# Queries of three kv groups by Strassen's scheme, and scores two steps ahead, in a decoder layer on one core

## The chip, the cores and the metric

The kernel runs on one core of one Trainium2 chip. The metric is device time in microseconds (us) of one execution. TensorE is called PE here, VectorE DVE, ScalarE ACT, GpSimd POOL, and SyncE, whose queue issues the DMAs, SP.

## The reference

One decoder layer on 8 sequences of 128 tokens with 512 channels: attention with 32 query heads in 8 kv groups of 4, cross attention with a context, and a gated feed-forward network (FFN) with 4-bit weights. Cut to what the change touches:

```python
def _L0_attn_ref(hidden_states, w_q, w_k, w_v, w_o):
    ...
    q = (hidden_states @ w_q).reshape(B, S, Hkv, g, D)      # 1024 x 512 @ 512 x 4096
    k = (hidden_states @ w_k).reshape(B, S, Hkv, D)
    v = (hidden_states @ w_v).reshape(B, S, Hkv, D)
    scores = jnp.einsum('bqhgd,bkhd->bhgqk', q, k) * scale
    ...
    probs = jax.nn.softmax(scores.astype(jnp.float32), axis=-1).astype(q.dtype)
    attn = jnp.einsum('bhgqk,bkhd->bqhgd', probs, v)
    attn = attn.reshape(B, S, Hq * D)
    return attn @ w_o
...
x = x + _L0_attn_ref(_layernorm(x, axis=-1), L0_attn_w_q, L0_attn_w_k, L0_attn_w_v, L0_attn_w_o)
```

All of it is float32.

## The kernel before

**Three products for one.** A float32 operand is held as two float16 tiles, a high part and the remainder. `split` (L117) makes them: ACT casts the high part, DVE or POOL subtracts it from the source. `mm3` (L160) then runs three matmuls per contraction block of 128: high x high, high x remainder, remainder x high. All accumulate in one PSUM bank.

**Tiling.** The 8 sequences make two halves of 4, that is of 512 tokens. The normalized input stands transposed in `hT`, four contraction blocks of 128 channels by 512 tokens for each half. Weights are fetched from memory per kv group in float32 into a raw tile (`rawq`, one buffer for all groups). ACT sums their squares (`sumsq`, L244), PE and DVE make a scale of it (`scales_parts`, L276). `convert` (L350) multiplies by the scale on POOL in place and splits the result, remainder on POOL.

**Queries.** `proj_q` (L497) computes one head of 128 rows for one half: 4 contraction blocks x 3 matmuls of 512 columns, 12 in all, into a bank of tag `j`; then `split` writes `qh` on ACT and `ql` on DVE. PSUM has two banks for each of four tags (L187): `j` for projections, `s` for scores, `a` for values, `o` for output projections.

**Steps.** A step is one kv group on one sequence; there are 64. A unit is one group on one half, 4 steps; 16 units run group by group (the last two groups take turns by halves). `step(i)` (L1365) issues, in this order:

- `att_s` (L587) for step i+1: 12 matmuls of scores, row maxima on DVE, exponentials on ACT, scaling on POOL (L622), the two float16 parts of the probabilities `pb` (ACT and POOL, L121), and a DMA that transposes `pb` to `pt`
- `proj_piece`: a fourth of the projections of the unit after the next one begun, that is one head's queries, and at times keys or values
- `att_o` (L653) for step i-1: 12 matmuls of 512 columns, then DVE adds the result to the residual `xr` (L662)
- `att_v` (L639) for step i: 5 matmuls of 256 columns with `pt`, then the split to `ah` (ACT) and `al` (DVE)

What else a step does comes from a table `todo`: fetches, sums of squares and weight conversions of later groups, each at a fixed step. Steps 8 to 42 also hold one chunk of the FFN's dequantization each (`dequant`, L785): two loads and two DVE instructions (L807, L811) that write the FFN weights `nf`. From step 43 the context is loaded and prepared, from step 53 another step function mixes in cross attention, and from step 60 the FFN.

**Order.** The order of instructions on each engine is made when the program is built, by a scheduler that follows these issues and some hand-set orders (`issue_after`, L124). Each engine then runs its own list in order; waits between engines are semaphores.

## Time and profile before

| what | us |
|---|---|
| timed runs | 659.69, 659.74, 661.82; median 659.74 |
| the profiled execution | 660.26 |
| its span, first to last instruction | 658.5 |
| PE busy | 631.9 |
| DVE busy | 465.0 |
| ACT busy | 440.0 |
| POOL busy | 378.5 |

The profile comes from one execution. Its lines name the source line, engine, operation and tiles (output <- inputs), and give the count, busy time, mean duration and what ended the idle time before. In lists over time the first number is the start and the second the duration, both in us from the span's start. Durations of matmuls overlap one another. The output projections of steps 8, 16, 24, 32 and 42 are added to `xr` at 117.4, 178.9, 238.3, 298.1 and 376.0 us, so these steps take 7.6 us in the mean.

### The profile page before, as it was taken

Reading aid. Unit: us, or ns where it says so; the run is one execution under the profiler, and the core shown is the slowest. Engines: PE = TensorE matmul, PEld = TensorE weight load, DVE = VectorE, ACT = ScalarE, POOL = GpSimd, SP = SyncE. Lnnn points to the kernel's source line nnn. Section 1 sums busy time; section 2 is a strip of 40 time slices with the busy share of each in tenths; the row PEclk is TensorE's granted clock in tenths of the full one; section 3 lists DMA queues with packets and bytes.
Section 4 is the critical chain, followed back from the end, with each engine's and each line's share of the span. In section 5 each row is a group of like instructions: output and inputs, shape, how many; then the busy total and the mean of one; then the engine's idle time right before and its main releaser. Section 6 shows DMA issues by size and latency. Waiting matters only on the chain.

```text
span 658.5 us, 12421 instructions
## 1 busy us (share of the span) xinstructions
PE 631.9 (96%) x3992; PEld 342.8 (52%) x3992; DVE 465.0 (71%) x1475; ACT 440.0 (67%) x1238; POOL 378.5 (57%) x586
## 2 busy tenths in 40 slices
PE   8799999999999999999999999989998988999996
PEld 5465545565655555555555554546554444445443
DVE  6756776666766777677768554757776768988986
ACT  5587678465658575666668566856566578867674
POOL 7757477563738693464678395724576247622521
PEclk9899999999999999999999999999999999999999
DMA  9277254945553766455455523333544253112002
GB/s 310 53 169 176 67 81 117 230 98 157 127 153 104 183 142 148 123 145 145 130 159 96 136 40 109 70 88 60 90 73 70 40 89 53 24 25 65 1 1 64
DMA packets 117773, 69.34 MB, mean 105 GB/s; under 512 B 84190, under 2 KB 100593, under 8 KB 117708
## 3 DMA queue, kind: packets, MB, share of 16 engines
q1 hardware_dynamic: 117708, 68.55, 44.2%
q8 instruction: 31, 0.51, 0.3%
q14 instruction: 34, 0.28, 0.2%
HBM read 42.12 MB, written 2.20 MB: 67 GB/s over the span
## 4 chain that ended last, share of the span: by engine, by line
PE 62%; DVE 10%; POOL 9%; ACT 8%; DMA 7%; issue 3%; SPq 1%; DVEq 0%; POOLq 0%; ACTq 0%
PE ps_c L1181 6%; PE ps_o L166 6%; PE ps_c L1182 6%; PE ps_o L164 6%; PE ps_o L165 6%; PE ps_q L164 5%; PE ps_q L166 5%; PE ps_q L165 5%; DMA pt<-pb 2%; POOL pb L121 2%; DMA rawq<-in_L_attn_w_q_dram 2%; POOL s L622 2%; ACT junk L262 2%; DVE ps_c L1194 2%; PE ps_k L165 1%
## 5 line engine op out<-in xcount | busy, mean ns | idle before, releaser
L565 ACT ACTIVATE s<-s,negm 128x64 f32<-128x64 f32 (+1 forms) x256 | 93.1, 365 | 41.1 <-DVE negm L608 40.8
L164 PE MATMUL ps_q<-hT,wqh 128*128 128x512 f16 (+1 forms) x260 | 97.7, 376 | 2.6 <-DVE ql L121 1.6
L164 PE MATMUL ps_o<-woh,ah 128*128 128x512 f16 x256 | 97.1, 379 | 3.0 <-ACT ah L118 3.0
L166 PE MATMUL ps_o<-woh,al 128*128 128x512 f16 x256 | 96.9, 379 | 1.1 <-DVE al L121 0.6
L166 PE MATMUL ps_q<-hT,wql 128*128 128x512 f16 (+1 forms) x260 | 97.7, 376 | 0.0
L165 PE MATMUL ps_q<-hT,wqh 128*128 128x512 f16 (+1 forms) x260 | 97.7, 376 | 0.0
L165 PE MATMUL ps_o<-wol,ah 128*128 128x512 f16 x256 | 97.0, 379 | 0.0
L662 DVE SCALAR_TENSOR_TENSOR xr<-ps_o,unsc,xr 128x512 f32<-128x512 f32 x64 | 47.9, 748 | 48.6 <-PE ps_o L166 46.0
L121 POOL TENSOR_TENSOR pb<-s,pb 128x256 f16<-128x256 f32 (+1 forms) x128 | 70.6, 566 | 17.9 <-ACT pb L118 15.5
L575 POOL TENSOR_SCALAR rec<-rec 128x4 f32<-128x4 f32 x64 | 15.2, 237 | 99.0 <-DVE rec L573 77.8
L608 DVE CUSTOM_DVE_ANT_0 s<-ps_sc,mask,soft 128x64 f32<-128x64 f32 (+1 forms) x256 | 67.3, 310 | 3.8 <-PE ps_sc L166 1.4
L121 DVE TENSOR_TENSOR ql<-ps_q,qh 128x512 f16<-128x512 f32 x64 | 44.0, 687 | 33.3 <-ACT qh L118 33.1
L622 POOL TENSOR_TENSOR s<-s,rec 128x128 f32<-128x128 f32 (+1 forms) x128 | 63.5, 517 | 4.7
L118 ACT CAST pb<-s 128x256 f16<-128x256 f32 (+1 forms) x128 | 42.8, 348 | 26.5 <-POOL s L622 24.7
L118 ACT CAST ah<-ps_at 128x512 f16<-128x512 f32 x64 | 37.3, 583 | 24.5 <-PE ps_at L166 9.7
L565 ACT ACTIVATION_READ_ACCUMULATOR s<-s,negm 128x1 f32 x256 | 48.0, 187 | 0.0
L121 DVE TENSOR_TENSOR al<-ps_at,ah 128x512 f16<-128x512 f32 x64 | 43.7, 683 | 4.7 <-ACT ah L118 4.4
L1194 DVE TENSOR_SCALAR ps_c<-ps_c,rTg 128x512 f32<-128x512 f32 (+1 forms) x56 | 40.7, 750 | 7.1 <-PE ps_c L1182 6.8
L118 ACT CAST qh<-ps_q 128x512 f16<-128x512 f32 x64 | 36.6, 572 | 11.7 <-PE ps_q L166 10.6
L1192 ACT ACTIVATE ps_c<-ps_c,rTu 128x512 f32<-128x512 f32 (+1 forms) x57 | 36.3, 660 | 11.3 <-PE ps_c L1182 9.3
L166 PE MATMUL ps_sc<-k,ql 128*128 128x128 f16 (+1 forms) x256 | 42.9, 207 | 0.5 <-DVE ql L121 0.5
L165 PE MATMUL ps_sc<-k,qh 128*128 128x128 f16 (+1 forms) x256 | 41.8, 207 | 0.0
(244 smaller groups left out, 1699.5 us busy)
## 6 DMA issues: line engine op xcount, KB each, us to landing
rawq<-in_L_attn_w_q_dram SPq DMA_DIRECT2D x8, 1024.0 KB
rawo<-in_L_attn_w_o_dram SPq DMA_DIRECT2D x8, 1024.0 KB, 5.8
zi<-zd SPq DMA_DIRECT2D x26, 256.0 KB, 4.1
vd<-v SPq DMA_DIRECT2D x64, 64.0 KB, 3.0
qr<-_L_ffn_down_qweight_dram SPq DMA_DIRECT2D x10, 256.0 KB
xr<-in_x_dram SPq DMA_DIRECT2D x8, 256.0 KB, 8.6
rawk<-in_L_attn_w_k_dram SPq DMA_DIRECT2D x8, 256.0 KB, 5.8
rawv<-in_L_attn_w_v_dram SPq DMA_DIRECT2D x4, 512.0 KB, 6.9
```

Of the source, the lines that this page charges most:

```text
L118: a = nc.scalar.copy(hi, src)
L121: b = (lo_eng or nc.vector).tensor_tensor(lo, src, hi, ALU.subtract)
L164: nc.tensor.matmul(ps, lh, rh, start=start and i == 0, stop=False)
L165: nc.tensor.matmul(ps, lh, rl, start=False, stop=False)
L166: nc.tensor.matmul(ps, ll, rh, start=False, stop=stop and i == n - 1)
L565: exp = nc.scalar.activation(v, v, AF.Exp, bias=negm[:, j : j + 1], scale=-1.0, accum_out=sums[:, j : j + 1],)
L608: nc.vector.tensor_tensor_reduce(view, flat(ps, cols[j]), masks[j // 2], soft_t[g][:, j % 2 : j % 2 + 1], BIG, ALU.add, ALU.min, negm,)
L622: mul = nc.gpsimd.tensor_tensor(v, v, rec[:, 2 * k : 2 * k + 2].unsqueeze(2).to_broadcast([P, 2, (k + 1) * HQ]), ALU.mult,)
L662: return nc.vector.scalar_tensor_tensor(xr[b], ps, unsc_t[g], xr[b], ALU.mult, ALU.add)
L1181: nc.tensor.matmul(ps, lh, rh, start=r == 0, stop=False, skip_group_check=r > 0)
L1182: nc.tensor.matmul(ps, lh, rl, start=False, stop=True, skip_group_check=r > 0)
L1194: nc.vector.tensor_scalar(ps, ps, sc, None, ALU.mult)
```

## The change

**Strassen's scheme.** For kv groups 3 to 5, two heads and one half are computed together. Weights of the two heads form a 2 x 2 block matrix (two heads by two halves of the contraction), the tokens another (two halves of the contraction by 256 tokens left and right). Eight block products become seven, in Winograd's form, on sums of weight blocks and sums of token blocks. Each block product is 2 contraction blocks x 3 matmuls of 256 columns.

- Token sums: `t_sum` makes four differences for each half, once, in steps 8 to 17, into new tiles `T0` and `T1` (DVE for the sum, `split` on ACT and POOL). They are built from a float32 copy of the tokens; that of half 0 is left from the start, that of half 1 is added up again from `hT` by two DVE adds.
- Weight sums: `fast_scale`, `fast_sums` and `fast_cast` work per pair of heads on POOL in place in `rawq`, with casts before and after: 3.5 tile pairs for two heads instead of 2. A plan `FPLAN` spreads them over 5 steps.
- The product itself, `fast_q`, comes in four stages over three steps. Two banks `A` and `B` of tag `j` are held. ACT copies a finished bank to SBUF and half of it back into the other bank, on which PE goes on accumulating; DVE adds twice from one bank half into another, and PE accumulates onto one of these sums.

**Order.** In steps 14 to 42 `att_s` and the projections run two steps ahead instead of one (step 14 issues both, step 42 none). Queries of the three groups are placed by hand before and after `att_o`; their keys and values use banks of tag `o`. Fetches of query weights for groups 3 to 5 come one step earlier than before relative to their use, and weight preparation of groups 3 to 7 is moved one step ahead.

**Memory.** Scratch tiles of the start (`hb`, `zw`, `z`, `srow`, `scol`) now lie inside the FFN weight tiles `nf`, which are filled later. No work is added by that.

The core of the diff:

```diff
+    def t_sum(half, n):
+        full = h32b if half else h32
+        b = [[full[:, 2 * r : 2 * r + 2, c * HH : (c + 1) * HH] for c in range(2)] for r in range(2)]
+        if half and n < 2:
+            ks = slice(2 * n, 2 * n + 2)
+            return nc.vector.tensor_tensor(
+                full[:, ks, :], hT[0][1][:, ks, :], hT[1][1][:, ks, :], ALU.add
+            )
+        dst, one, two, i = (
...
+        ins = nc.vector.tensor_tensor(dst, one, two, ALU.subtract)
+        split(tT[half][:, 0, i], tT[half][:, 1, i], dst, nc.gpsimd)
...
+    def fast_sums(g, p, part):
...
+        tt = nc.gpsimd.tensor_tensor
+        if part == 0:
+            issue_after(tt(a22, a21, a22, ALU.add), pace["mul"])
+            tt(a21, a11, a21, ALU.subtract)
+        else:
+            issue_after(tt(a11, a22, a11, ALU.subtract), pace["mul"])
+            tt(a12, a12, a11, ALU.subtract)
...
+        A = bank("j", [P, TH], "ps_q")
+        m5 = term(A[:, right], Z1, 2, summed(0), True)
+        term(A[:, left], X, 0, tok(0, left), behind=m5)
+        B = bank("j", [P, TH], "ps_q")
+        u = B[:, left]
+        both = work.tile([P, TH], F32, name="s5", tag="s5", bufs=1)
+        nc.scalar.copy(both, A)
+        s5 = both[:, right]
+        nc.scalar.copy(u, both[:, left])
+        yield
+        term(A[:, left], X, 2, tok(2, left))
+        term(u, Z0, 0, summed(1))
+        nc.vector.tensor_tensor(A[:, right], u, s5, ALU.add)
+        yield
+        term(u, Z1, 0, summed(2))
+        nc.vector.tensor_tensor(B[:, right], u, s5, ALU.add)
+        term(A[:, right], Z0, 2, tok(2, right))
+        put_q(g, half, 2 * p, A)
+        yield
+        term(u, Y, 2, summed(3))
+        put_q(g, half, 2 * p + 1, B)
...
+        for p in range(2):
+            i = HB * u - 7 + 2 * p
...
+            place(slot_b, i, go[p])
+            place(slot_b, i + 1, go[p])
+            place(slot_a, i + 2, go[p])
+        place(slot_a, HB * u - 4, lambda g=g, half=half: run(proj_k(g, half, place="o")))
...
+    SOON, BACK = 14, 42
+
     def step(i):
         g, b = steps[i]
-        if i + 1 < len(steps):
+        if i <= SOON or i > BACK:
             att_s(*steps[i + 1])
-        proj_piece(*divmod(i + 1 + HB, HB))
+            proj_piece(*divmod(i + 1 + HB, HB))
+        if SOON <= i < BACK:
+            att_s(*steps[i + 2])
+            proj_piece(*divmod(i + 2 + HB, HB))
+        for f in slot_a.pop(i, ()):
+            f()
         after = att_o(*steps[i - 1]) if i else None
+        for f in slot_b.pop(i, ()):
+            f()
         att_v(g, b)
```

`term(ps, w, k0, rhs)` runs the six matmuls of one block product: two contraction blocks from `k0`, three matmuls each.

## The prediction

> **What bounds the kernel now.** I read four views: the busy shares and slices of the page, the busy times by stage, the timeline of the matmuls, and PE's waits. The profiled execution took 660.26 us, 658.5 of it span. The median of the three timed runs is 659.74; I work against the profile and take 0.5 off at the end.
>
> The page first. PE is near full in every slice until the last third, at full granted clock.
>
> ```profile
> PE 631.9 (96%) x3992; PEld 342.8 (52%) x3992; DVE 465.0 (71%) x1475; ACT 440.0 (67%) x1238; POOL 378.5 (57%) x586
> PE   8799999999999999999999999989998988999996
> PEclk9899999999999999999999999999999999999999
> ```
>
> The stages that the change touches, in busy us (instructions):
>
> ```profile
> 103.00:163.00 60.00, 59.96 (x402) 33.62 (x401) 38.71 (x130) 38.20 (x125) 35.55 (x58) 1.00 0.60 145
> 163.00:223.00 60.00, 60.00 (x399) 33.52 (x397) 40.09 (x139) 39.42 (x129) 39.49 (x62) 1.00 0.54 134
> 223.00:283.00 60.00, 60.00 (x400) 33.57 (x399) 40.96 (x135) 38.13 (x125) 35.73 (x59) 1.00 0.63 152
> 283.00:344.00 61.00, 60.72 (x411) 34.10 (x410) 43.29 (x140) 40.00 (x129) 39.25 (x61) 1.00 0.50 135
> ```
>
> The columns are PE, PEld, DVE, ACT, POOL. PE is full, the others two thirds. But a PE duration overlaps the next one, so full by this count is not yet proof. The timeline settles it (start, duration):
>
> ```profile
> 300.40 0.27 PE L164 MATMUL ps_v<-wvh,hT 128*128 128x256 f16 x1
> 300.51 0.27 PE L165 MATMUL ps_v<-wvl,hT 128*128 128x256 f16 x1
> ...
> 302.49 0.38 PE L165 MATMUL ps_q<-hT,wqh 128*128 128x512 f16 x1
> 302.71 0.38 PE L166 MATMUL ps_q<-hT,wql 128*128 128x512 f16 x1
> ```
>
> What a matmul costs is the step to the next start. Twelve 512-column ones start over 2.37 us (302.28 to 304.65), 0.2155 each; ten 256-column ones over 0.98 (299.75 to 300.73), 0.109 each, every one with a new weight. I summed such steps over the matmuls' sizes and held them against the clock: from 100 to 300 us they fill all but some 0.3 us; from 145 to 436 us about 6 us are missing, 4.9 of them after 376. So in steps 8 to 42 PE's own work is the time, nearly to the last tenth. PE's waits agree:
>
> ```profile
> PE ps_o L164 <- ACT ah L118: 3.0, 3, 1.7
> PE ps_at L645 <- DMA pt<-pb: 1.9, 4, 0.8
> PE ps_q L164 <- DVE v L545: 1.0, 1, 1.0
> ```
>
> Three, four and one waits in the whole run.
>
> **What the change removes on PE.** Three groups, two halves, two pairs of heads make 12 pairs. A pair was 2 x 12 matmuls of 512 columns; it becomes 7 products x 6 matmuls of 256. Off go 288 x 0.2155 = 62.1 us; on come 504 x 0.109 = 54.9. Net 7.2 us, all in a stage where PE has no gap. The built order confirms the counts (288 fewer of 512, 504 more of 256, no other matmul changed), and from step 52 on PE's order is that of before.
>
> The Trainium skill, page "TensorE: Matmul & The Clock Gate", section "Back-to-back issue gap", speaks against this: in streams of weight load and matmul it gives some 81 ns at 128 columns and 131 at 512; halfway (98 at 256, my interpolation) the change would lose 504 x 0.098 - 288 x 0.131 = 11.7 us. The trace has 0.2155 at 512 and 0.109 at 256, which fits the same section's formula for an isolated gap, so I don't follow the 131.
>
> **What it adds elsewhere** (built order for counts, rows of the profile for durations):
> - ACT: 12 copies of a whole bank out of PSUM (row of 128x512 from PSUM, 0.58) 7.0; 12 copies of 256 back into PSUM (128x256 cast, 0.37) 4.5; 6 more casts of 128x512 (0.62) and 6 of 128x256 (0.40) for the weights, 6.1; 8 casts of token sums, 4.9. Together 22.5 us.
> - DVE: 24 adds of 256 with one PSUM input (128x256 row, 0.42) 10.1; 6 token sums (0.72 at 512; two of 1024, about 1.4) 5.7. Together 15.8.
> - POOL: 24 weight sums in place (256-element row, 0.63) 15.1; 12 more weight remainders (6 x 1.20, 6 x 0.68) 11.3; 8 token remainders (1.17) 9.4. Together 35.8.
> - SP: not one DMA more (287 rows in both). The weight fetch of a group moves one step ahead, and waits for POOL's last reading of the one raw buffer; behind it in SP's queue stand the transposes of the probabilities and the dequantization loads.
>
> None of this runs on PE. Its cover is the idle third of the three engines. The token sums lie in steps 8 to 17, the rest in some 185 us (steps 17 to 42). POOL gets 26 us there, from about 63% to 79% (26 less work time of PE counted); ACT goes from 65% to about 76%, DVE from 68% to about 74%. On average everything fits. Were the cover gone, POOL's 26 us would be the price.
>
> It is uneven, though. Summing POOL's rows between the score steps in the built order, eight steps around 17 to 24 hold 53.5 us against some 59 of PE's work, and four in a row 31 against 30; before, the same eight held 41. The heaviest 20 us of before, 320 to 340, had POOL busy 18.6 of 20 and PE without a gap, so such a burst can be carried. Scores two steps ahead give one step more, some 7 us, for POOL, DMA and the softmax; that is the cover for the burst. In time by itself it gives little: the 0.3 us wait for a transpose at 302, perhaps 1.5 us in all with the gaps around 374.
>
> A second effect of a busier POOL is on DVE:
>
> ```profile
> 299.20 1.33 POOL L121 TENSOR_TENSOR wql<-rawq,wqh 128x512 f16<-128x512 f32 x1
> ...
> 299.55 1.52 DVE L811 SCALAR_TENSOR_TENSOR nfd<-qi,zi 128x512 f16<-128x512 int32 x1
> 310.33 0.69 DVE L811 SCALAR_TENSOR_TENSOR nfd<-qi,zi 128x512 f16<-128x512 int32 x1
> ```
>
> The same dequantization step takes 0.69 us alone and 1.52 beside a POOL subtraction. With some five to ten more such meetings DVE loses 3 to 8 us, off the path. The Trainium skill, "SBUF — State Buffer", section "Who interferes with whom", gives the reason (a DVE instruction with two SBUF inputs and a GpSimd one that reads SBUF block each other); by its rule the 24 new adds, with one input in PSUM, stay free, and the token sums do not. I count nothing on PE for either.
>
> **What it adds as waits on PE.** Each pair hands over three times: PE to ACT and back (first two products, then the copies), PE to DVE and back twice. A handover takes what a matmul runs past its step (0.27 - 0.11 = 0.16), the copy (0.58) or add (0.42) and a signal: about 0.8 and 0.65 us if the engine is free, and more by what stands ahead of it in order. In the built order I added PE's own work between producer and consumer: 2 to 5 us nearly everywhere, but 0.6 and 0.7 in two of the copies and 0.5 in one add, and 1.2 to 1.8 in a few. The matmul that waits holds all of PE behind it. With a free engine that is 0.1 to 0.3 us at three places, 0.5 us; with one instruction of 0.6 ahead at six places, some 4 us. Nothing bounds it better: queue lengths at those points are not in this trace. The same kind of handover (queries to scores, values to outputs) costs PE under 2 us in steps 8 to 42 of before, so I take 2.5, from a range of 0.5 to 7.
>
> Behind step 42, six gaps worth 5 us up to 436 us (at 391, 410, 427, 434 and smaller) hang on ACT behind loads of the context and on the preparation of groups 6 and 7, which moves one step. I take them as they are, within 2 either way. From there PE's order is unchanged and follows earlier.
>
> **Sum.** 660.3 - 7.2 - 0.5 (gaps that the lead closes) + 2.5 = 655.1 by the profile, 654.5 by the median.
>
> **Rivals.**
> 1. *New waits eat the gain* (chance 0.24): 5 to 9 us of handovers and late POOL results. For it: in-order engines at 76%, three short distances, bursts on POOL. Against: the near absence of such waits before at similar bursts. 657 to 661; say 659.
> 2. *POOL becomes the bound* (0.10), the slower side. Place: the eight steps of each group's weight preparation. It decides once POOL, with its waits for ACT's casts between its subtractions, can't be busy over about 85% there: 53.5 / 0.85 = 63 us against 59. At 80% it is 67, 8 us lost in the densest eight steps, and about 3 in each of the two others of 44 to 48 us with their own bursts: 659.7 - 7.2 + 14 = 666. For it: over 60 us no stage showed POOL over 44. Against: the 93% over 20 us.
> 3. *The change does less than it says* (0.03): a 256-column matmul costs more than half of a 512 one. By the duration columns (0.379 and 0.273) the change would add 504 x 0.273 - 288 x 0.379 = 28 us. The steps between starts speak against it, on every row of 256.
> 4. *More than forecast* (0.08): handovers cost nothing and the lead also fills the gaps after 376: 7.2 + 2 to 3, 650.
>
> Forecast case 0.55, 652 to 656.4.
>
> **The numbers.** A measurement of this kernel can tell about 0.5%, 3.3 us, from no change. Under 656.4 lie the forecast case, rival 4 and a few hundredths of rival 1: 0.66. Within 3.3 us: most of rival 1 and the mildest of rival 2: 0.25. Slower: the rest of rivals 2 and 3, 0.09. The range takes in rival 4 and rival 1: 650.5 to 661.
>
> **What would show it.** Right: 504 new matmuls at 0.109 us from start to start; the four 60-us windows still full on PE; the end of the last output projection 5 us earlier; POOL near 75 to 80% between 190 and 370 us. Wrong: PE waits on the copy into ps_q, on the adds, or on pt with over 4 us in total (rival 1); gaps of PE that end with POOL or with transposes behind POOL around steps 16 to 24 (rival 2); steps of 256 above 0.12 (rival 3).

## The result, and the profile after

The changed kernel takes **667.71 us** (median of four runs, 667.46 to 669.19) against 659.72 (four runs, 659.36 to 661.82) of the kernel before: a ratio of 1.0125, interval 1.0109 to 1.0140. The forecast was 654.5 in a range of 650.5 to 661, so the sign was wrong too.

The profiled execution after has a span of 665.7 us (658.5 before). The page of the kernel after, in its first rows:

```profile
PE 628.3 (94%) x4208; PEld 364.2 (55%) x4208; DVE 489.1 (73%) x1509; ACT 455.7 (68%) x1282; POOL 424.0 (64%) x630
...
PE   8799999989999989999997799999998988999996
```

PE does less and takes longer. Its row of slices (16.6 us each), nines without a break from 33 to 428 us before, has holes now: eights at 133 and 233 us and two sevens from 349 to 383 us. The stages, same windows and columns as before (PE, PEld, DVE, ACT, POOL, then the granted clock):

```profile
103.00:163.00 60.00, 57.79 (x390) 32.30 (x389) 44.91 (x141) 40.27 (x130) 44.53 (x65) 1.00 0.48 121
163.00:223.00 60.00, 58.04 (x431) 37.09 (x429) 49.26 (x140) 41.91 (x130) 52.61 (x71) 1.00 0.58 147
223.00:283.00 60.00, 56.17 (x477) 40.65 (x474) 41.99 (x140) 41.84 (x137) 45.42 (x70) 1.00 0.54 135
283.00:344.00 61.00, 60.96 (x478) 41.11 (x477) 45.37 (x149) 44.69 (x140) 50.04 (x73) 1.00 0.62 151
344.00:380.00 36.00, 28.50 (x211) 17.55 (x209) 23.21 (x71) 19.16 (x65) 21.27 (x32) 0.95 0.47 132
380.00:440.00 60.00, 60.00 (x407) 33.56 (x406) 37.27 (x156) 45.94 (x149) 42.96 (x66) 1.00 0.27 67
```

Three of the four windows that were full are short by 2 to 4 us, the stretch 344 to 380, at a clock of 0.95, by 7.5; the one from 380 on is full. In the kernel before these last two windows were

```profile
344.00:380.00 36.00, 35.43 (x234) 19.04 (x232) 25.49 (x92) 25.14 (x83) 21.92 (x35) 1.00 0.54 119
380.00:440.00 60.00, 55.89 (x377) 30.56 (x376) 35.05 (x147) 40.62 (x124) 41.25 (x63) 1.00 0.34 82
```

The saving itself came: the timeline of PE in a product of the kernel after has

```profile
203.86 0.27 PE L603 MATMUL ps_q<-hT,wql 128*128 128x256 f16 x1
203.97 0.38 PE L603 MATMUL ps_q<-hT,wqh 128*128 128x256 f16 x2
204.19 0.27 PE L603 MATMUL ps_q<-hT,wql 128*128 128x256 f16 x1
204.30 0.19 PE L164 MATMUL ps_sc<-k,qh 128*128 128x64 f16 x1
```

that is four 256-column matmuls in 0.44 us, 0.11 each.

For all that follows I sum PE's **gaps**: the time between the starts of matmuls in excess of what their columns take (0.2157, 0.109, 0.0557 us for 512, 256, 128). PE's own work fell from 626.2 to 619.5, by some 7 (7.2 by the counts); the gaps rose from 25.5 to 39.5, by 14. (The two levels depend on what the few float32 matmuls of the start are taken for; the differences and the table don't.) By place:

| gaps of PE in us | 100 to 200 | 200 to 380 | 380 to 460 | 100 to 460 |
|---|---|---|---|---|
| before | 0.3 | 1.3 | 5.7 | 7.3 |
| after | 4.8 | 15.3 | 0.3 | 20.4 |

PE's waits, kernel after:

```profile
PE ps_at L770 <- DMA pt<-pb: 10.4, 11, 3.2
PE ps_o L166 <- DVE al L121: 2.9, 5, 1.8
...
PE ps_o L164 <- ACT ah L118: 1.7, 2, 1.1
...
PE ps_sc L166 <- DVE ql L121: 1.5, 2, 1.0
...
PE ps_q L603 <- DVE ps_q L629: 1.3, 2, 0.9
```

DVE's adds of the new handovers (`ps_q`, last row) hold PE for 1.3 us, and this view has no row of a wait on ACT's copies. What holds it for ten is `pt`, the transposed probabilities, 1.9 before; they come at the end of the longest chain (scores, DVE, ACT, POOL, ACT and POOL, SP, DMA). The chain that ended last shows what lies in it, here across the worst gap of the kernel after:

```profile
355.10 0.64 DVE xr L787
355.74 2.04 DVE qi L932
357.78 0.60 DVE ql L121
358.38 3.09 DVE nfd L936
361.46 0.10 DVE rec L698
361.56 0.28 SPq L924
...
361.95 6.29 DMA rawo<-in_L_attn_w_o_dram
```

`qi` and `nfd` are the two DVE instructions of a chunk of the FFN's dequantization. Free they take 0.48 and 0.69 us; here 2.12 and 3.16 by the timeline. Behind them stand DVE's evictions; SP's queue held a load (L924) whose buffer `nfd` frees, then a 1-MB weight fetch, and only then the transpose, whose `pb` was ready at 360. It landed at 368.9, 6.4 us after its issue; the median of those whose landing the profile tells is 3.0. PE waited 3.2 us, until 369.0, and behind the gap its clock was halved, from about 371 to 374.4: a 512-column matmul started every 0.43 us.

### The profile page after: what moved, and what is told of

Its sections match the earlier page's. It is cut to its first block, busy times and chain, and to the rows that moved or that the text cites. A ratio compares the mean times of both kernels' runs of the same rounds, so it can differ in the third digit from the quotient of the medians.

```text
span 665.7 us, 13013 instructions
## 1 busy us (share of the span) xinstructions
PE 628.3 (94%) x4208; PEld 364.2 (55%) x4208; DVE 489.1 (73%) x1509; ACT 455.7 (68%) x1282; POOL 424.0 (64%) x630
## 4 chain that ended last, share of the span: by engine, by line
PE 41%; POOL 18%; DVE 11%; ACT 11%; DMA 10%; issue 8%; SPq 0%; DVEq 0%; POOLq 0%; ACTq 0%
PE ps_c L1349 6%; PE ps_c L1350 6%; PE ps_q L603 4%; PE ps_o L164 4%; PE ps_o L166 4%; PE ps_o L165 3%; POOL pb L121 3%; DMA pt<-pb 3%; POOL s L747 3%; DMA rawo<-in_L_attn_w_o_dram 3%; ACT junk L263 2%; POOL wql L121 2%; ACT s L690 2%; DMA rawq<-in_L_attn_w_q_dram 2%; POOL wol L121 2%
## 5 line engine op out<-in xcount | busy, mean ns | idle before, releaser
L121 POOL TENSOR_TENSOR pb<-s,pb 128x256 f16<-128x256 f32 (+1 forms) x128 | 73.4, 589 | 21.9 <-ACT pb L118 20.2
L747 POOL TENSOR_TENSOR s<-s,rec 128x128 f32<-128x128 f32 (+1 forms) x128 | 65.2, 529 | 3.7
L700 POOL TENSOR_SCALAR rec<-rec 128x4 f32<-128x4 f32 x64 | 15.5, 243 | 77.3 <-DVE rec L698 71.9
L164 PE MATMUL ps_q<-hT,wqh 128*128 128x512 f16 (+1 forms) x164 | 61.3, 374 | 2.4 <-DVE ql L121 1.6
L165 PE MATMUL ps_q<-hT,wqh 128*128 128x512 f16 (+1 forms) x164 | 61.3, 374 | 0.0
L166 PE MATMUL ps_q<-hT,wql 128*128 128x512 f16 (+1 forms) x164 | 61.3, 374 | 0.0
L121 POOL TENSOR_TENSOR wql<-rawq,wqh 128x512 f16<-128x512 f32 (+1 forms) x40 | 43.6, 1098 | 8.4 <-PE ps_q L603 4.6
L118 ACT CAST qh<-ps_q 128x512 f16<-128x512 f32 x64 | 36.8, 576 | 11.4 <-PE ps_q L166 8.4
L166 PE MATMUL ps_sc<-k,ql 128*128 128x64 f16 (+1 forms) x256 | 42.5, 207 | 1.5 <-DVE ql L121 1.5
```

The costliest lines, as they stand in the source:

```text
L118: a = nc.scalar.copy(hi, src)
L121: b = (lo_eng or nc.vector).tensor_tensor(lo, src, hi, ALU.subtract)
L164: nc.tensor.matmul(ps, lh, rh, start=start and i == 0, stop=False)
L165: nc.tensor.matmul(ps, lh, rl, start=False, stop=False)
L166: nc.tensor.matmul(ps, ll, rh, start=False, stop=stop and i == n - 1)
L747: mul = nc.gpsimd.tensor_tensor(v, v, rec[:, 2 * k : 2 * k + 2].unsqueeze(2).to_broadcast([P, 2, (k + 1) * HQ]), ALU.mult,)
```

## The experiments

Eighteen kernels, each against the kernel before on the same chip; times are medians. Nothing of the result is left out where nothing is said.

**1. Scores one step ahead, Strassen's scheme kept**

```diff
-    SOON, BACK = 14, 42
+    SOON, BACK = 1000, 1000
```

> The changed kernel with scores and projections one step ahead throughout, as before; Strassen's products, the sums and the earlier weight preparation stay. Changed kernel 667.7 us, before 659.7. Theory A (bunches): the two-step lead, with a unit's queries ready only one step before, makes PE issue scores in bunches of four with pauses of 12 to 20 us, so POOL and ACT stand idle and are then overrun; without it 653 to 657 us, and the pauses between the reciprocals of scores stay under 13 us. Theory B (load): the added work of POOL, DVE and ACT is itself the price; 664 to 670. Theory C (one blocked queue): the 10 us lost at 356 to 374 us come from one late fetch ahead of a sum of squares on ACT; 657 to 662 if that doesn't recur.

685.31 us, ratio 1.0361 (1.0326 to 1.0397), above all three ranges. Gaps from 100 to 460 us: 37.7. The lead is no burden; without it Strassen's scheme costs 25 us.

**2. The lead alone**

```diff
-    FAST = range(3, 6)
+    FAST = range(0)
-    t_steps = {8 + i: ((0, i),) if i < 4 else ((1, i - 4),) for i in range(10)}
+    t_steps = {}
```

> The two-step lead alone: no group uses Strassen's scheme, no token sums, plain query projections at 512 columns; the earlier weight preparation stays. Theory A (bunches): the lead does harm by itself, 661 to 665 us, with pauses of over 13 us between the reciprocals of scores. Theory B (load): nothing is added to POOL, DVE or ACT, 658 to 660.5. Theory C (one blocked queue): 658 to 661.

655.48 us, ratio 0.9918 (0.9892 to 0.9944): faster than both kernels, and below all three ranges. This kernel keeps the earlier weight preparation besides the lead, for groups 6 and 7 too; no run tells the two apart. The stages of this kernel around the former gaps:

```profile
344.00:380.00 36.00, 34.51 (x238) 18.94 (x235) 24.05 (x90) 25.49 (x80) 25.38 (x37) 1.00 0.55 145
380.00:440.00 60.00, 59.71 (x388) 32.83 (x386) 36.78 (x156) 41.64 (x133) 38.33 (x60) 1.00 0.37 84
```

PE was busy 55.89 of the last 60 us before, and is 59.71 now, in a window that lies behind step 42, where the lead is over. Gaps: 2.9. So Strassen's part costs 12 us in time: 7 saved on PE, 18 us of new gaps by the spans (654.3 to 665.7). The rest looks for these.

**3. Two sums of squares of group 6 one step later**

```diff
-        at(m + 1, lambda g=g: sumsq("o", g, 0, 0, 2))
-        at(m + 2, lambda g=g: sumsq("o", g, 1, 0, 2))
+        late_o = g == 6
+        at(m + 1 + late_o, lambda g=g: sumsq("o", g, 0, 0, 2))
+        at(m + 2 + late_o, lambda g=g: sumsq("o", g, 1, 0, 2))
```

> The changed kernel, but the two sums of squares of group 6's output weights come one step later on ACT, so that ACT is not held by the fetch of rawo. Theory C (one blocked queue): the gap at 356 to 374 us goes, with it the stretch at half clock, 658 to 661 us. Theory A (bunches) and theory B (load): the time is lost elsewhere in the same stretch, 663 to 667.

669.97 us, ratio 1.0140 (1.0102 to 1.0179), above every range. The gap at 366 us stays (3.37), by the same way: `nfd` 3.17, the load, the fetch, the transpose. ACT no longer stood there; the wait for the fetch on ACT was no cause.

**4 to 6. Side work taken away step by step.** Kernel 4 leaves out the weight sums on POOL; kernel 5 the sums and the two extra casts too; kernel 6 the token sums as well, so that the products read plain tokens. All three keep products, handovers and places, and leave out what makes the result right.

```diff
+        if True:
+            return                  # kernel 4: first lines of fast_sums
...
+        if name in ("Y", "Z0"):     # kernel 5: fast_cast, besides
+            return
-        X, Y, Z0, Z1 = (s_w[g, p, n] for n in ("X", "Y", "Z0", "Z1"))
+        X, Y, Z0, Z1 = (s_w[g, p, n] for n in ("X", "Z1", "X", "Z1"))
...
-            return tT[half][:, 0, i], tT[half][:, 1, i]
+            return tok(2 * (i % 2), left)   # kernel 6, besides; t_steps = {}
```

> The changed kernel without the 24 in-place weight sums on POOL (some 15 us of POOL work): the products then run on unsummed weights, so that part of the computation is left out. Theory B (load): POOL was overrun, 660 to 664 us. Theory A (bunches): 665 to 668, as the pauses stay. Theory C (one blocked queue): 664 to 668 unless the late fetch goes too.

> The changed kernel, but with the weight work of before: two tile pairs for two heads instead of 3.5, and no weight sums; the seven products run on them, so the weights' part of Strassen's scheme is left out. Known: changed kernel 667.7 us, lead alone 655.5, so the scheme costs 12 us net, 19 over PE's saving. Theory S (side work: weights and token sums hold up the in-order queues of ACT, POOL and DVE, and the softmax behind them): 652 to 660 us. Theory H (handovers of a pair's bank between PE, ACT and DVE): 663 to 668. Theory P (place: the products stand in three steps by hand, so scores come in bunches): 663 to 668.

> As the run with plain weight work, and also no token sums: the products read the tokens themselves; left out is all of Strassen's additions outside the bank. What is left is the seven products with their copies and adds. Theory S: 647 to 652 us, PE's saving under the lead's 655.5. Theory H: 660 to 668. Theory P: 660 to 668.

674.57, 666.85 and 665.84 us; ratios 1.0221 (1.0183 to 1.0258), 1.0105 (1.0076 to 1.0133), 1.0082 (1.0060 to 1.0104). Taking 15 us of work off POOL made the kernel slower by 7, above every range for it. With no side work at all (kernel 6) it is 2 us better than the changed kernel, in the ranges of theories H and P and far from that of S, and the gaps from 200 to 380 us stay at 14.9. POOL's load is not what makes them. (In kernel 6 those from 100 to 200 are gone: 0.0.)

**7. All side work, plain queries**

```diff
-            return
+            for i in range(2):
+                wq_t[g * GH + 2 * (j // 2) + i] = s_w[g, j // 2, ("X", "Z1")[i]]
...
-        if g not in FAST:
-            continue
+        continue
```

> The reverse: all weight and token work of Strassen's scheme on ACT, POOL and DVE, under the two-step lead, but queries by plain matmuls of 512 columns with one tile pair per head (for every second head a summed one, so that part of the computation is changed). Theory S: 662 to 675 us, lead alone plus most of the 19. Theory H and theory P: 655 to 659.

661.96 us, ratio 1.0027 (0.9998 to 1.0055), between the two ranges; `X` and `Z1` hold sums here, so the result is another. From 200 to 380 us this kernel and then the changed one:

```profile
200.00:380.00 180.00, 179.34 (x1182) 98.51 (x1180) 120.89 (x420) 121.76 (x391) 140.08 (x209) 1.00 0.56 141
```

```profile
200.00:380.00 180.00, 168.35 (x1328) 113.88 (x1326) 130.40 (x408) 121.74 (x388) 135.33 (x201) 0.99 0.56 140
```

POOL, the last busy column, has 140 us in the first and 135 in the second, and PE is full in the first. The side work makes gaps only from 100 to 200 us (3.8).

**8. Side work and products, no handovers.** ACT's copies and DVE's adds are left out; the partial sums start bank halves of their own, so the result lacks terms.

```diff
-        both = work.tile([P, TH], F32, name="s5", tag="s5", bufs=1)
-        nc.scalar.copy(both, A)
-        s5 = both[:, right]
-        nc.scalar.copy(u, both[:, left])
...
-        term(u, Z0, 0, summed(1))
-        nc.vector.tensor_tensor(A[:, right], u, s5, ALU.add)
+        term(u, Z0, 0, summed(1), True)
...
-        nc.vector.tensor_tensor(B[:, right], u, s5, ALU.add)
...
-        term(u, Y, 2, summed(3))
+        term(B[:, right], Y, 2, summed(3), True)
```

> The changed kernel without the 24 copies on ACT and 24 adds on DVE inside fast_q: the seven products start or go on in four bank halves of their own, so the recombination is left out. Theory H: 650 to 657 us. Theory S: 662 to 667, some 21 us of ACT and DVE work less but the weights still in the queues. Theory P: 662 to 668.

663.80 us, ratio 1.0051 (1.0033 to 1.0068): 3.9 under the changed kernel, and by the time in the ranges of S and P, not of H. Gaps from 200 to 380 us: 6.1 in place of 15.3.

**9. Products alone, no handovers.** Kernel 6 with the edit of kernel 8.

> Strassen's 504 matmuls at their hand-set places, but nothing beside them: no token sums, no weight sums (the products read plain casts and plain tokens, which leaves out the sums that make the result), and no copies and adds between the products (every partial sum starts a bank half of its own). PE's own work is that of the changed kernel, 620; ACT, DVE and POOL carry slightly less than before. Theory H (the handovers cost, since the same kernel with handovers had a span of 664.1): PE's gaps fall back to the 21 of the lead alone, span 648 to 650, time some 650. Theory P (the places cost: two banks of tag j held over three steps, keys and values in the banks of the output projections): gaps stay above 32, span 656 to 662. Theory N (neither alone, they add): gaps of 26 to 31, span 652 to 655.

659.65 us, ratio 0.9983 (0.9967 to 1.0000); gaps 11.4, of which 8.8 from 200 to 380 us. Neither of the simple cases; the handovers and what is left both cost.

**10. Places and banks alone.** Kernel 6 with 24 plain matmuls of 512 columns for each pair of heads, in the same four stages:

```diff
+        m5 = term(A, X, 0, tok(0, full), True)
+        B = bank("j", [P, TH], "ps_q")
+        yield
+        term(A, X, 2, tok(2, full), behind=m5)
+        yield
+        m6 = term(B, Z1, 0, tok(0, full), True)
+        put_q(g, half, 2 * p, A)
+        yield
+        term(B, Z1, 2, tok(2, full), behind=m6)
+        put_q(g, half, 2 * p + 1, B)
+        yield
```

> No Strassen product: each pair of heads is computed plainly with 24 matmuls of 512 columns, but in the same four stages, at the same hand-set places, in the same two held banks, with keys and values in the banks of tag o. No side work. Nothing of the result is left out. PE's own work is that of before, 626. Theory P (the places cost): gaps above 30, span over 661. Theory H (the handovers do): gaps of 21 to 24 as with the lead alone, span 654 to 657, time 655 to 658. Theory N: in between, span 657 to 661.

661.19 us, ratio 1.0004 (0.9989 to 1.0018): 5.7 over the lead alone, with a span of 660.3 as theory N had it. Gaps 7.0: one of 2.9 at 378 us, where PE waits for DVE's scale of a later group's weights, half clock from 382.0 to 385.4 behind it, and one of 1.6 at 435. So most of these gaps stand behind 376 us, where the changed kernel has next to none.

**11. The lead alone, up to step 52**

```diff
-    SOON, BACK = 14, 42
+    SOON, BACK = 14, 52
```

(on kernel 2)

> The lead alone, kept up to step 52 in place of 42; nothing left out. If the lead's gain comes from room between the scores and their transposes wherever PE is the limit, the gaps after step 42 (some 8 us of PE's gaps lie between 376 us and the cross attention) close in part: 652 to 654. If they come from the loads of the context that share the queue with the transposes there, or if the lead only helps beside the dequantization, it stays at 655 to 656.

657.38 us, ratio 0.9952 (0.9936 to 0.9968). No better than up to 42, and above both ranges.

**12 to 14. Three moves in the whole changed kernel:** ACT's copies get a step of time; the copies run on DVE; the lead begins at step 8.

```diff
-            place(slot_b, i, go[p])
+            place(slot_a, i + 1, go[p])
```

```diff
-        nc.scalar.copy(both, A)
+        nc.vector.tensor_copy(both, A)
-        nc.scalar.copy(u, both[:, left])
+        nc.vector.tensor_copy(u, both[:, left])
```

```diff
-    SOON, BACK = 14, 42
+    SOON, BACK = 8, 42
```

> The changed kernel whole; only the second of the four stages of a pair of heads stands one step later, ahead of the next output projection in place of behind this one, so that ACT's two copies have about 7 us of PE's work to get done in, not the 2.6 of one output projection; the DVE add behind it has 2.6 in place of 7. Theory T (the handovers cost because the copies have too little time, and the chains behind them in ACT's queue run late): the gaps of PE between 200 and 380 us fall from 15 to 9 or less, span 657 to 661, time 659 to 663. Theory W (ACT stands still in its queue for the product itself, wherever the copy is placed): no change within 2 us, 666 to 669. Rival: the add becomes the late one, with PE waits on it over 3 us: 668 to 672.

> The changed kernel whole; the two handover copies of each pair run on DVE in place of ACT. Theory A (ACT's queue is where the handover hurts, since its casts of queries and attention outputs stand behind a copy that waits for PE): the gaps fall by 3 to 6, 661 to 665. Theory D (any engine that evicts in order is held as long, and DVE is the fuller one): DVE's own list, with the row maxima and remainders, is held in the same way, and the time rises to 669 to 675.

> The changed kernel whole; the lead of two steps begins at step 8 in place of 14, so that it stands over the token sums of steps 8 to 17 too. Theory: the 4 to 5 us of gaps that PE has between 100 and 200 us come with the token sums and the first weight sums (they are there with the side work alone and gone without it), and a step more of room covers them: gaps there fall to 1 or 2, time 664 to 665. Rival (the lead can't cover them, since the late transposes there come from a late weight fetch that holds ACT in its queue): within 1 us of 667.7.

669.34, 670.49 and 671.50 us; ratios 1.0146 (1.0108 to 1.0184), 1.0145 (1.0126 to 1.0164), 1.0191 (1.0131 to 1.0251). Gaps 22.1, 23.8 and 24.5: none helps. It was neither the time that the copies have, nor ACT's queue as such, nor the lead missing in steps 8 to 14. Kernel 12 lies within 2 us of the changed kernel, as theory W had it, and kernel 13 in the range of theory D, with 5.3 us of PE's waits on the copies that DVE now makes and 3.5 on an add; kernel 14 missed both its ranges. The gaps moved, and the sum stayed.

**15 to 17. One group, two groups, and the token sums alone**

```diff
-    FAST = range(3, 6)
+    FAST = range(3, 4)    # kernel 15; range(3, 5): 16; range(0): 17
```

> The changed kernel with Strassen's scheme for group 3 alone; groups 4 and 5 are computed plainly, lead and token sums stay. PE's work is 2.4 us under that of the lead alone (span 654.3). Theory E (each group brings its own gaps, some 4 us, on top of 4 for the token sums): 658 to 661. Theory L (two thirds of the gaps behind 200 us lie at 340 to 375, in the third group, where the weight fetches crowd; the first two cost about what they save): 655 to 658.

> The same for groups 3 and 4, group 5 plain. PE's work is 4.8 us under that of the lead alone. Theory E: 660 to 664, halfway from one group to three. Theory L: 654 to 658, the best of the versions with Strassen's scheme, perhaps ahead of the lead alone (655.5).

> The lead alone, with the token sums of steps 8 to 17 made and not used; nothing of the result is left out. PE's work is that of before. If the gaps of 100 to 200 us (4.8 in the changed kernel, 3.8 with all side work, none with the lead alone) belong to the token sums: 3 to 4 us there, span 657 to 659. If they belong to the first weight sums and casts, which start at step 14: under 1 us there, span as with the lead alone, 654 to 655.

664.20, 670.22 and 660.27 us; ratios 1.0084 (1.0051 to 1.0117), 1.0135 (1.0097 to 1.0173), 0.9991 (0.9968 to 1.0013). One group already costs 4 us over the token sums, though PE saves 2.4; two cost 10, by the intervals as much as three. Kernels 15 and 16 lie above the ranges of both theories. No share of the scheme beats the lead alone, and the third group is not the place where it is lost. The profile of kernel 15 is of an execution of 670.7 us: three of its ten took 670.4 to 671.1, the other seven 662.9 to 664.4, with the same built order. The token sums cost 4.8 us over the lead alone, most of what the side work of kernel 7 costs (6.5). Only 2.6 us of that are gaps between 100 and 200 us.

The traces show what the large gaps have ahead of them. Kernel 15, timeline of POOL, DVE and PE:

```profile
244.33 1.05 POOL L121 TENSOR_TENSOR pb<-s,pb 128x128 f16<-128x128 f32 x2
245.35 1.15 POOL L121 TENSOR_TENSOR wql<-rawq,wqh 128x512 f16<-128x512 f32 x1
246.46 1.05 POOL L121 TENSOR_TENSOR pb<-s,pb 128x128 f16<-128x128 f32 x2
247.47 1.15 POOL L121 TENSOR_TENSOR wql<-rawq,wqh 128x512 f16<-128x512 f32 x1
```

```profile
244.46 4.36 DVE L932 TENSOR_SCALAR qi<-qr,sh 128x352 int32<-128x352 int32 x1
248.85 0.53 DVE L936 SCALAR_TENSOR_TENSOR nfu<-qi,zi 128x352 f16<-128x352 int32 x1
249.29 0.42 DVE L632 TENSOR_TENSOR ps_q<-ps_q,s 128x256 f32<-128x256 f32 x1
```

```profile
245.66 0.38 PE L165 MATMUL ps_o<-wol,ah 128*128 128x512 f16 x1
249.77 0.58 PE L603 MATMUL ps_q<-T,wqh 128*128 128x256 f16 x2 [3.73 <-DVE ps_q L632]
```

POOL runs from 244.33 to 248.6 without a pause, six instructions with two inputs each (a row with x2 merges two). DVE's decoding instruction `qi`, begun 0.13 us later, ends when that run ends. Behind it on DVE stands the add for which PE's next product waits: a gap of 3.9 us, and half clock from 249.1 to 252.5. The spread of `qi` in the kernel before, the lead alone and the copies on DVE (minimum, median, maximum in ns of 35):

```profile
L807 DVE TENSOR_SCALAR qi<-qr,sh x35: 392/478/1242, 114.6 to 366.9; 128x512 int32<-128x512 int32 x26, 128x352 int32<-128x352 int32 x8, 96x512 int32<-96x512 int32 x1
```

```profile
L932 DVE TENSOR_SCALAR qi<-qr,sh x35: 393/545/1422, 114.7 to 364.6; 128x512 int32<-128x512 int32 x26, 128x352 int32<-128x352 int32 x8, 96x512 int32<-96x512 int32 x1
```

```profile
L932 DVE TENSOR_SCALAR qi<-qr,sh x35: 388/596/4975, 114.7 to 385.6; 128x512 int32<-128x512 int32 x26, 128x352 int32<-128x352 int32 x8, 96x512 int32<-96x512 int32 x1
```

The medians are near each other; the longest is four times as long. Over both decoding instructions the longest is under 1.75 us in the kernel before and in kernels 2, 7, 10 and 11, none of which has half a microsecond of gaps between 200 and 360 us, and 2.0 to 5.0 in every kernel with Strassen's products. Kernel 17, without them, has one of 3.47 at 167.6 us and one large gap, 2.04 at 172.7, on `al` behind it on DVE. That goes together everywhere; by itself it doesn't say which comes first.

Nor is a POOL run enough for it. In the 19 traces with decoding, 305 of these instructions start inside an unbroken run of two-input POOL instructions that has over 2 us to go. Of these 287 were done in under 1.75 us, ahead of the run's end, and 18 ended 0.2 to 0.6 us behind it; none lies between. In the changed kernel it is 19 to 1. Here is one of the 19, `qi` on DVE and what POOL does beside it, two inputs each and no pause:

```profile
242.71 0.91 DVE L932 TENSOR_SCALAR qi<-qr,sh 128x352 int32<-128x352 int32 x1
```

```profile
242.69 0.73 POOL L586 TENSOR_TENSOR rawq<-rawq 128x256 f32<-128x256 f32 x1
243.38 1.25 POOL L121 TENSOR_TENSOR wql<-rawq,wqh 128x512 f16<-128x512 f32 x1
244.59 1.25 POOL L747 TENSOR_TENSOR s<-s,rec 128x128 f32<-128x128 f32 x2
245.81 1.05 POOL L121 TENSOR_TENSOR pb<-s,pb 128x128 f16<-128x128 f32 x2
```

What decides whether DVE gets in after one POOL instruction or only after the last, no run shows.

**18. The changed kernel without decoding on DVE.** Both DVE instructions are left out and one fill stands for them, so the FFN's weights are constant; the loads stay.

```diff
-        qi = deqp.tile([P, H], I32, name="qi", tag="qi", bufs=1)
-        ins = nc.vector.tensor_scalar(
-            qi[:p, :n], qr[:p, :n], sh[:p], 15, ALU.logical_shift_right, ALU.bitwise_and
-        )
-        issue_after(ins, after)
-        nc.vector.scalar_tensor_tensor(
-            nf[m][:p, g, c0:c1], qi[:p, :n], -1.0, zi[:p, :n], ALU.add, ALU.subtract
-        )
+        issue_after(nc.vector.memset(nf[m][:p, g, c0:c1], 1.0), after)
```

> The changed kernel, but the two DVE instructions that decode each chunk of the FFN weights are left out, one DVE fill with a constant in place of them; the loads stay. All of Strassen's scheme, its side work, its handovers and its places stay. Theory K: the long chains come from the decoding instruction on DVE, which is not let in while POOL runs one two-input instruction after another: it takes 3 to 5 us in place of 0.5 in each kernel with large gaps (4.36 with one group, 3.79 with the products alone, 3.47 with the token sums alone, 4.97 with copies on DVE), never over 2 in the kernel before or with the lead alone, and what evicts for PE stands behind it on DVE. Then PE's gaps from 100 to 380 us, 20 in the changed kernel, fall to 8 or less, span 653 or less. Rival: these are symptoms of bunches that come from the handovers themselves: the gaps stay over 13, span 658 or more. In between, both. The kernel before has 1.6 us of gaps there, so this edit in itself can't bring more than that.

690.78 us, ratio 1.0466 (1.0448 to 1.0483): as a whole the experiment failed. With no reader to hold their buffers the loads no longer wait; all are issued between 112 and 197 us (111 to 355 before), and the transposes behind them come late (one gap of 10.7 us at 171). Of use are the windows behind that:

```profile
160.00:220.00 60.00, 41.79 (x286) 25.36 (x284) 21.98 (x75) 26.82 (x84) 34.16 (x50) 0.86 0.85 190
220.00:280.00 60.00, 60.00 (x481) 41.60 (x479) 40.44 (x150) 45.70 (x151) 50.81 (x83) 1.00 0.37 97
280.00:340.00 60.00, 60.00 (x501) 42.42 (x500) 38.45 (x141) 43.34 (x141) 42.04 (x68) 1.00 0.33 70
340.00:380.00 40.00, 36.05 (x285) 24.10 (x284) 24.97 (x97) 26.82 (x89) 23.65 (x39) 1.00 0.17 37
```

From 220 to 360 us, with products, handovers and side work all there, PE has 0.5 us of gaps. The same steps run some 20 us earlier in the changed kernel, and have 5.3 us there. So the gaps of the middle need the decoding or its loads; which of the two, this run doesn't tell. But from 374 us PE has 7 us of gaps again without any decoding, in the steps of the changed kernel's worst place. POOL shows what precedes them:

```profile
372.58 0.22 POOL L700 TENSOR_SCALAR rec<-rec 128x4 f32<-128x4 f32 x1 [15.56 <-DVE rec L698]
```

It had nothing to do for 15.6 us, since no scores came, and then has three steps' work at once. The changed kernel has the same at 340 us, a pause of POOL of 9.0 us ahead of the run that held `qi` and `nfd`. That led to the last reading.

**Across all traces: PE's own order.** Scores are the start of the chain that ends in `pt`. I took, from the order of matmuls on PE alone, how much of PE's own work (columns only, no gap counted) lies between the ends of one step's scores and the next's, in the steps from 190 to 372 us. The mean is 6.4 to 7.5 us in all kernels; the spread is not the same:

| kernel | spread (standard deviation) us | longest us | gaps of PE 200 to 380, us |
|---|---|---|---|
| 11, lead to 52 | 1.6 | 9.9 | 2.5 |
| 10, places alone | 1.7 | 10.7 | 2.8 |
| 7, side work alone | 1.8 | 12.8 | 1.3 |
| 17, token sums alone | 1.8 | 12.8 | 1.4 |
| 2, lead alone | 1.9 | 12.8 | 2.2 |
| before | 2.4 | 11.4 | 1.3 |
| 9, products, no handover | 2.5 | 12.7 | 8.8 |
| 8, the same with side work | 2.6 | 12.7 | 6.1 |
| 15, one group | 3.5 | 13.9 | 9.7 |
| 18, no decoding on DVE | 5.0 | 20.9 | 11.9 |
| 16, two groups | 5.0 | 17.3 | 11.9 |
| 13, copies on DVE | 5.3 | 19.4 | 18.6 |
| 6, products with handovers | 5.4 | 20.9 | 14.9 |
| **after** | 5.5 | 17.2 | 15.3 |
| 3 and 14 | 5.5 | 17.1, 17.2 | 15.2, 15.5 |
| 5, plain weight work | 5.9 | 19.4 | 15.0 |
| 12, copies a step | 6.1 | 19.6 | 17.4 |
| 4, no weight sums | 7.5 | 32.3 | 20.4 |
| 1, one ahead | 8.6 | 29.7 | 24.3 |

Over the whole table the gaps rise with the spread, in kernels of quite different content; kernel 4, slower with less work, has its place too. This order is fixed when the program is built, so it can't be a result of the gaps. Three things limit the reading. Up to 2.6 the gaps don't follow the spread (1.3 us in the kernel before, 8.8 in kernel 9). Every kernel with handovers stands at 3.5 or more and every one without at 2.6 or less, so outside kernels 1 and 4 the table can't tell the spread from other effects of the handovers. And kernel 18 has such an order too (5.0), yet loses its 11.9 us at the ends, behind the crowded loads and from 374 us on: between 220 and 360 us it has 0.5 us of gaps at a spread of 3.9 and a longest distance of 14.0, where kernel 15 with 3.5 and 13.9 has 9.7. (The order is its own: in the same steps the changed kernel has 4.8 and 16.4.) So an order as uneven as kernel 15's made no gaps there by itself; it took the decoding or its loads beside it. In the kernel after, scores of successive steps end on PE at 321.8, 329.4, 345.7, 346.3, 350.2 and 350.7 us: nothing for 16 us, then four steps within five. With the lead alone they end at 319.8, 326.1, 334.9, 341.2, 347.5 and 351.5. Where PE computes two steps' scores in a row, ACT, POOL and the transposes get double portions after a pause; the lead of two steps, some 15 us, is used up by a hole of 16.

## Why the prediction was wrong, step by step

**PE's saving: right.** 0.109 us from start to start, 6.8 us less by the records, 7.2 by the counts.

**The lead, "0.5" put in: wrong by 4 us, to the good.** With the earlier weight preparation it brought 4.5 us in time. The gaps behind step 42, which I took as they were, went from 5.7 to 0.6 us. That is where the lead has ended and groups 6 and 7 are prepared a step earlier, so which of the two closed them stays open.

**"I take 2.5, from a range of 0.5 to 7" for waits on PE: the step that failed.** I looked at how long PE would wait on the copies and adds themselves. That stayed small (1.3 us in the row above). All else that the scheme does to PE I put at nothing, and all of it came to some 18 us of gaps over the lead alone, most of them waits on `pt` and on evictions by DVE. Part of it goes with what the handovers do to the order: in the built order of PE other work stands between the stages, and the scores of the next steps, which were spaced by 2.4 us around their mean, are spaced by 5.5. The ladder in times, each against the one before: lead alone 655.5; places and banks (kernel 10) +5.7; products in place of plain matmuls (kernel 9) -1.5, that is 7.2 saved and 5.7 lost; handovers (kernel 6) +6.2, with the spread going from 2.5 to 5.4; side work (the change) +1.9. Only the 6.2 come with a rise of the spread; the 5.7 of the places and the 5.7 lost by the products come at spreads of 1.7 and 2.5. The order of the rungs matters: over the lead alone the side work by itself costs 6.5. Nor do the rungs stand in the changed kernel as they are: most of kernel 10's gaps lie behind 376 us, where the changed kernel has 0.3. Sum 12.2, where the forecast had -4.7 for all but the lead. The spread can be read off the built order; I had counted PE's work between handovers and POOL's between score steps there, and took the score steps as regular.

**"None of this runs on PE", cover by the idle third: right as a count, wrong as a cost.** The averages held: POOL 75% between 200 and 380 us, as forecast, and fuller (78%) in kernel 7, with 1.3 us of gaps. So rival 2 (POOL becomes the bound, 666) came near the time by another way, which is luck. That an idle third covers added work only while the work comes evenly is how I read it; it is not shown by itself.

**"Such meetings ... off the path. I count nothing on PE": wrong, as a second link.** I saw `nfd` go from 0.69 to 1.52 beside one POOL subtraction and took the length of a meeting as bounded by it. It mostly is, but not always: now and then (18 of the 305 above) DVE stays out to the end of an unbroken run of two-input POOL instructions, 2 to 5 us, and evictions for PE are queued behind on DVE. The Trainium skill, "SBUF — State Buffer", section "Who interferes with whom", also names the form of `qi`, `tensor_scalar`, among those that can contend with GpSimd, when the operands meet its conditions; I had applied only its rule of two inputs. It says that whoever issues first gets the shared ports for the whole instruction, which accounts for one POOL instruction; that DVE can stay out over six (4.36) or more (4.97) in a row is what the traces here add. A DVE instruction with one PSUM input, `ql` at 357.70 in the changed kernel, kept its 0.68 us beside such a POOL instruction, as the page has it.

**"SP gets not one DMA more": right, and beside the point.** One transpose behind one 1-MB fetch, held by a buffer that a late DVE instruction frees, made the largest gap.

**Rival 1** (new waits eat the gain, 659) had the right kind: `pt` over 4 us was its sign, and it is 10.4. It was bounded by 9 us; measured against the lead alone, 18 us of gaps came.

**What stays open.** That handovers and the rest of the scheme cost this time is shown by leaving them out; how they cost it is argued. That the spread of the scores makes the gaps is read from twenty orders and traces, and kernel 18 shows that it is not enough by itself; no kernel was run that keeps the products and forces even scores, which would test it. No kernel has the lead without the earlier weight preparation. Products without handovers have 6 to 9 us of gaps at a spread hardly above that of before (kernels 8 and 9); that part, and the 5.7 us of the places alone with their wait on a weight scale at 378 us, are measured and not explained. That long decoding makes single gaps longer is shown by where it stands, ahead of the largest gap in kernels 13, 15 and 17 and on the chain of the change's worst; no run kept DVE from being shut out and left the loads as they were. That executions of kernel 15 differ by 7 us at one built order says that the order doesn't settle the time. The ladder compares medians of different calls, whose runs of the kernel before lay between 659.7 and 661.2.

## What to carry to other kernels

Where PE is the limit and feeds a long chain in pieces, read off the built order how evenly it issues the start of that chain, before any cost is summed: here a distance of 16 us, over the some 15 of a two-step lead, stood ahead of the largest gap, and shares of busy time didn't show it. The wait on each new handover was 1.3 us in all and did not tell what the handovers cost (3.9 and 6.2 us by leaving them out). A change that bundles a cheap reordering with a costly algorithm is worth taking apart: the two-step lead, with the earlier weight preparation, gives 655.5 us, the best kernel of this study, and the scheme it was to cover takes 12 back.

## What the runs showed of the hardware that was not expected

- A DVE instruction of 0.4 us (`qi`, 128x352, int32) took 4.36 and 4.97 us beside unbroken runs of two-input POOL instructions of as much (kernels 15 and 13) and ended only 0.2 us behind the run's end. Beside another such run, with 5.2 us to go, it took 0.91 (kernel after, at 242.7).
- A transpose of 128 x 768 issued half a microsecond behind a 1-MB fetch on the same queue landed after 6.4 us; the median is 3.0.
- PE's clock was halved for some 3.4 us behind a gap of 3.3 us (a 512-column matmul each 0.43 us, from 2 us behind the gap's end), and for 3.4 us, from 1 us behind its end, after one of 2.9 us in kernel 10. With PE at work throughout, such a stretch costs 1.7 us on top of the gap (an estimate: half of 3.4). The Trainium skill, "TensorE: Matmul & The Clock Gate", section "HAM oscillation — how this bites in real kernels", puts the limit for idle gaps at about 3.4 us. Here the length of one gap didn't decide: in kernel 3 one of 2.1 us at 137 us was followed by half clock, in kernel 15 four in a row of 0.4 to 1.1 us from 234 on, and in kernel 9 one of 3.3 us at 368 was not.
